# Moving the last block's first stages between two feed-forward stages, and splitting late weight sums, in a fast-multiplication transformer block

## The chip, the cores and the metric

The kernel runs on one core of a Trainium2 chip. A core has five engines, each with a queue of its own that it works through in order: TensorE (PE, matrix products; its weight loads are the rows PEld), VectorE (DVE), ScalarE (ACT), GpSimd (POOL) and SyncE (SP, which here only issues DMAs). Engines wait for each other by semaphores. Arithmetic is in float32. The metric is the device time of one execution in microseconds (us).

## The reference

The input `x` is 2 rows of 2048 tokens with 512 features, and a condition vector for each row. The condition gives six vectors for each row (shift, scale and gate of two sub-layers):

```
emb = silu(t) @ ada_w + ada_b
shift_msa, scale_msa, gate_msa, shift_mlp, scale_mlp, gate_mlp = split(emb, 6)
norm = _ln(x) * (1 + scale_msa) + shift_msa
h = gelu(norm @ ssm_w1 + ssm_b1)            # exact gelu, 512 -> 512
x = x + gate_msa * (h @ ssm_w2 + ssm_b2)    # 512 -> 512
norm2 = _ln(x) * (1 + scale_mlp) + shift_mlp
hf = gelu(norm2 @ ff_w1 + ff_b1)            # tanh gelu, 512 -> 1024
x = x + gate_mlp * (hf @ ff_w2 + ff_b2)     # 1024 -> 512
```

## The kernel before

**Tiles and stages.** The 4096 tokens are cut into 8 blocks of 512 tokens (`NBLK`), four for each row of `x` (`PER_B`). A block goes through four products, which I call stages: hA (norm 1 times ssm_w1, class `First`), oA (times ssm_w2, `residual`), hC (norm 2 times ff_w1, `Second.products`) and oC (times ff_w2, `residual_in_leaves`). hA(7) is that stage of block 7, the last.

**Fast multiplication.** hA and oA are done as 2x2 blocks with seven products instead of eight, P1 to P7, in the order P1 P5 P6 P2 P7 P3 P4 (`CARRIED`); each has eight matmuls of 128x256. The operands of some products are sums: four sums make a "second operand" or a "first operand" (`sums_of_second`, `sums_of_first`, all recorded at line 348). nS is such a set from the normed input of hA, hSA from hA's output, hSC from hC's output, fw_t from the ff weight. hC has 26 products (`HK_P`) over 20 "forms", sums of blocks of the normed input (`sums_of_registers`, L919). oC cuts most of its seven products once more into seven "leaves" (rounds R0 to R6), whose operands are further sums: sums24, sums35, sums7 (`leaf_sums`) and the leaves of the weight (`leaves_of_weight`: P23, P4, P5, P7). A product's result in PSUM is added to its place by DVE (L735 in oA, L785 and L834 in oC, L998 in hC) or first copied by ACT (L995 in hC). A PSUM bank is used again only after it was read: that is how PE comes to wait for DVE or ACT. Biases get into PSUM ahead of the products by ACT copies ("seeds", L445 and L447).

**Norms.** A norm of a block is a chain over five engines: statistics (DVE, L512 and L513, four pieces), scales (POOL, eight small operations, L548 to L566, the last gives `nmr`), four normals (ACT, L580), four turns (DVE transposes into `blocks`, L591), 16 DMAs of 64 KB that finish the transpose (`move`, L600), and four modulates (ACT, L623, from `moved`). Norm 1 works in the place of x, so x is loaded again (`load_x`, L203) for the residual.

**The order of the work** is written out by hand. `hook(hooks, places, ops)` puts operations of the other engines behind a named product of a stage (behind product number n in hC); each engine then does them in that order:

```
    def hook(hooks, places, ops):
        for n, op in enumerate(ops):
            hooks.setdefault(places[min(n, len(places) - 1)], []).append(op)
```

With the order `CARRIED` the places of oA and hA are named by position: P1, P2, P6, P5, P7, P3, P4 mean behind the first, second, ... seventh product. The hooks of a stage stand in the queues between what the stage's own products need, so a sum that is hooked into oA stands ahead of the adds that follow it.

**The loop** (L1285 on) runs over i = 1 to 7. For each i it does, in PE's order: hC(i), oA(i+1), oC(i), hA(i+2); what would belong to a block past the last is left out. Block 7 therefore has hA(7) after oC(5), oA(7) after hC(6), and hC(7), oC(7) at the end. For block i+2, norm 1's normals are hooked at products 15, 17, 19, 21 of hC(i), its turns two products later, its moves at 23 (all on SP), its modulates behind the fifth product of oA(i+1), its nS sums in oC(i) on POOL. For block i+1, norm 2 runs through oA(i+1) (statistics), and oC(i) (scales, normals, turns, moves half on SP and half on ACT, modulates), and its 20 forms are made by POOL after oC(i), beside hA(i+2). In the iteration i = 6 there is no hA(8): the forms of block 7 are hooked late into oC(6) (`late_form`), the first six on DVE and 14 on POOL, and two of the four modulates are POOL's.

**Weights.** The ff weight is multiplied by the row's gate (`weight_of_second`, fold L396) and its sums are formed. For the first row, eight of its sums (`later`) are made by DVE inside oA(2) in the iteration i = 1. When the second row begins, in iteration i = 3, the weight is loaded again in two halves (`load_half`), folded by DVE in hA(5), and summed by DVE and POOL in hA(5), hC(4), oA(5) and oC(4).

**Storage.** Tiles of 1 MB (`big_tile`) come from a pool of seven; x, the normed inputs, hA, hClo and hChi are such tiles.

## Time and profile before

| | |
|---|---|
| three timed runs | 592.53, 594.62, 594.88 us; median 594.62 |
| the profiled execution | 594.65 us, its span 592.9 us |
| mean granted TensorE clock | 0.996 |
| PE busy | 582.0 us |
| DVE, ACT, POOL busy | 415.1, 261.9, 434.4 us |
| steady iterations (start of hA to start of hA) | 193.16, 262.33, 331.48: 69.17 and 69.15 us |
| the iteration with the new weight | 331.48 to 402.06: 70.58 us |
| the next | 402.06 to 471.22 (start of hA(7)): 69.16 us |
| hC(7) starts | 541.66 us |
| PE's last product ends | 588.3 us |

The profiled execution lies at the median. Its trace gives each instruction of each engine with its start and duration in microseconds from the span's start, and in brackets how long the engine stood idle before it and what ended the wait. A row such as `x8` joins eight instructions that follow each other; its duration then runs to the end of the last, which overlaps the next row a little, because matmuls are pipelined. A line number is that of the line which recorded the instruction; a helper such as L348 serves many tiles, so the names of the output and the input tiles tell which sums they are.

### The profile page before, as it was taken

To read this page: it belongs to the slowest core of one execution; us is meant where nothing else is said; L and a number is where in the kernel's file an instruction comes from. 1 tells how busy PE (TensorE), PEld (TensorE's weight loads), DVE (VectorE), ACT (ScalarE), POOL (GpSimd) and SP (SyncE) were. 2 spreads that over 40 slices of the span, in tenths; PEclk is the share of its full clock that TensorE was granted. 3 is DMA by queue.
4 is the path that set the end of the run, shared out by engine and by line. 5 is a ranking of instruction groups with operands and counts; after the bars stand their busy time and mean duration, and the time that the engine had idled before them with its cause. 6 is when DMAs were issued, how large, how long until landed. Compare 5 with 4: busy or idle time off the path is not lost.

```text
span 592.9 us, 9491 instructions
## 1 busy us (share of the span) xinstructions
PE 582.0 (98%) x3303; PEld 517.3 (87%) x3303; DVE 415.1 (70%) x750; ACT 261.9 (44%) x477; POOL 434.4 (73%) x522
## 2 busy tenths in 40 slices
PE   9999999999989999999999999999999999998996
PEld 5888888888879888998889988898889988897896
DVE  4978888897867365685756578874665626587666
ACT  2234457305533546435742588226474255312430
POOL 1875359999976938969788789997679693755460
PEclk9999999999989999999999999999999999999999
DMA  8990333302305402372033820233120420013002
GB/s 318 395 384 10 86 72 82 98 36 106 72 2 143 153 9 62 99 221 81 2 89 69 287 72 22 51 85 149 52 53 19 127 89 0 1 32 111 1 1 71
DMA packets 25243, 56.49 MB, mean 95 GB/s; under 512 B 4672, under 2 KB 5740, under 8 KB 23532
## 3 DMA queue, kind: packets, MB, share of 16 engines
q1 hardware_dynamic: 21472, 51.15, 26.9%
q10 hardware_dynamic: 3724, 4.75, 3.3%
q8 instruction: 26, 0.43, 0.3%
q14 instruction: 21, 0.17, 0.1%
HBM read 32.80 MB, written 8.40 MB: 69 GB/s over the span
## 4 chain that ended last, share of the span: by engine, by line
PE 83%; DVE 8%; DMA 4%; issue 1%; POOL 1%; ACTq 1%; ACT 1%; SPq 0%; DVEq 0%; POOLq 0%
PE px_hC L981 9%; PE py_hA L475 9%; PE py_oA L475 8%; PE py_hC L981 7%; PE py_oC L774 7%; PE pv_hC L981 7%; PE pl_oC_P_y L820 6%; PE pv_hA L475 4%; PE pl_oC_P_v L820 4%; PE pv_oA L475 4%; PE py_oC L475 2%; PE py_hC L475 2%; DMA ada<-in_L_cond_ada_w_dram 2%; PE pl_oC_P_x L820 2%; PE px_oA L475 2%; PE px_hA L475 2%
## 5 line engine op out<-in xcount | busy, mean ns | idle before, releaser
L348 POOL TENSOR_TENSOR hSC<-hClo,hChi 128x512 f32<-128x512 f32 (+1 forms) x17 | 20.4, 1207 | 42.1 <-ACT hChi L976 24.7
L623 ACT ACTIVATE nT<-nT,mod,mod 128x512 f32<-128x512 f32 x30 | 22.0, 803 | 56.0 <-DMA nT<-blocks 32.5
L919 POOL TENSOR_TENSOR forms<-forms 128x256 f32<-128x256 f32 x55 | 40.8, 741 | 4.7 <-DVE forms L919 1.5
L512 DVE BATCH_NORM_STATS2 st<-x 128x6 f32<-128x512 f32 x60 | 40.6, 676 | 5.1 <-DMA x<-in_x_dram 4.8
L981 PE MATMUL py_hC<-forms,fw 128*128 128x256 f32 x168 | 41.1, 380 | 0.4 <-DVE hClo L998 0.4
L998 DVE TENSOR_TENSOR hClo<-hClo,py_hC 128x512 f32<-128x512 f32 x42 | 28.5, 685 | 15.7 <-ACT hClo L995 9.7
L580 ACT ACTIVATE nT<-x,nmr,rstd 128x512 f32<-128x512 f32 x32 | 24.0, 806 | 35.1 <-POOL nmr L566 35.1
L981 PEld LDWEIGHTS py_hC<-forms,fw 128*128 128x128 f32 x168 | 31.8, 190 | 5.2 <-DVE hClo L998 0.8
L591 DVE STREAM_TRANSPOSE blocks<-nT 128x512 f32<-128x512 f32 x32 | 22.3, 707 | 18.8 <-ACT nT L580 18.8
L623 ACT ACTIVATE x<-x,mod,mod 128x512 f32<-128x512 f32 x24 | 17.6, 803 | 37.5 <-DMA x<-blocks 37.5
L998 DVE TENSOR_TENSOR hChi<-hChi,pv_hC 128x512 f32<-128x512 f32 x35 | 23.2, 681 | 9.8 <-PE pv_hC L981 8.1
L919 POOL TENSOR_TENSOR forms<-nT,forms 128x256 f32<-128x256 f32 x39 | 28.6, 754 | 1.0 <-DVE forms L919 0.5
L981 PE MATMUL px_hC<-forms,fw 128*128 128x256 f32 x112 | 27.9, 380 | 0.1
L976 ACT ACTIVATE hClo<-hClo,colsT 128x256 f32<-128x256 f32 x56 | 25.3, 499 | 5.0 <-DVE hClo L998 4.8
L475 PE MATMUL py_oA<-w,hA 128*128 128x256 f32 x112 | 26.5, 380 | 0.5 <-DVE x L735 0.5
L834 DVE TENSOR_TENSOR x<-pl_oC_P_y,x 128x256 f32<-128x256 f32 (+1 forms) x66 | 24.7, 375 | 2.4 <-PE pl_oC_P_y L820 0.9
L735 DVE TENSOR_TENSOR x<-py_oA,x 128x512 f32<-128x512 f32 x26 | 17.8, 686 | 11.8 <-PE py_oA L475 11.3
L976 ACT ACTIVATE hChi<-hChi,colsT 128x256 f32<-128x256 f32 x56 | 25.1, 497 | 1.9 <-DVE hChi L998 1.9
L774 PE MATMUL py_oC<-fw,hClo 128*128 128x256 f32 x112 | 26.0, 386 | 0.0
L995 ACT ACTIVATE hClo<-px_hC 128x512 f32<-128x512 f32 x21 | 12.5, 597 | 30.2 <-PE px_hC L981 25.8
L697 DVE TENSOR_TENSOR hA<-py_hA,hA 128x512 f32<-128x512 f32 x7 | 4.8, 690 | 30.0 <-PE py_hA L475 19.2
L774 PE MATMUL py_oC<-fw_s,hSC 128*128 128x256 f32 x112 | 25.3, 379 | 0.0
(340 smaller groups left out, 1792.8 us busy)
## 6 DMA issues: line engine op xcount, KB each, us to landing
x<-in_x_dram SPq DMA_DIRECT2D x13, 1024.0 KB
out_dram<-x SPq DMA_DIRECT2D x14, 512.0 KB
ada<-in_L_cond_ada_w_dram SPq DMA_DIRECT2D x6, 1024.0 KB
x<-blocks SPq DMA_DIRECT2D x96, 64.0 KB
nT<-blocks SPq DMA_DIRECT2D x72, 64.0 KB
fw<-in_L_cond_ff_w_dram SPq DMA_DIRECT2D x2, 2048.0 KB
nT<-blocks ACTq DMA_DIRECT2D x56, 64.0 KB
w<-in_L_cond_ssm_w_dram SPq DMA_DIRECT2D x3, 1024.0 KB
```

The lines of the kernel that those rows point to most:

```text
L475: nc.tensor.matmul(ps[b][j * apart][:, j, :], lhs(p, j, k), rhs(p, j, k), start=(fresh and j * (not apart) == 0 and k == 0), stop=(p in (" ...
L512: nc.vector.bn_stats(st, xs[self.i][:, c, :])
L580: nc.scalar.activation(t, x_c, AF.Identity, bias=self.nmr[:, c : c + 1], scale=self.rstd[:, c : c + 1])
L591: nc.vector.transpose(self.bl[:, :, :, c, :].rearrange("p m k q -> p k m q"), self.nT[:, c, :].rearrange("p (k m q) -> p k m q", k=KD, m=C),)
L623: nc.scalar.activation(dst, src, AF.Identity, bias=shift, scale=scale)
L774: yield lambda j=j, k=k: nc.tensor.matmul(ps[BANK[p]][:, j, :], hops(p, j, k), wops[p][:, k, :], start=False, stop=(k == kdim - 1), skip_g ...
L820: nc.tensor.matmul(t[:, n, :], hops.leaves[p][f][:, k, :], leaf_wops[p][f][:, k, :], start=room not in started, stop=(f in ("P2", "P3", "P ...
L834: nc.vector.tensor_tensor(d, src, d, ALU.add)
L919: eng.tensor_tensor(reg[d], reg[a], reg[b], ALU.add if f == "+" else ALU.subtract)
L976: nc.scalar.activation(h, h, AF.Gelu_apprx_tanh, bias=fb1T[:, m : m + 1])
L981: nc.tensor.matmul(ps[b][:, j, :], fa[ra][:, j * P : (j + 1) * P], fb[rb].rearrange("p a (c q) -> p c a q", q=Q), start=(fresh and j == 0) ...
L998: nc.vector.tensor_tensor(dest(d), dest(d), ps[b], op)
```

## The change

1. In iteration i = 5 (`ahead`), hA(7) is put between oA(6) and oC(5), and oA(7) between oC(5) and hC(6). PE's order is then hC(5), oA(6), hA(7), oC(5), oA(7), hC(6), oC(6), hC(7), oC(7). With it, norm 1 of block 7 moves: normals at products 9, 11, 13, 15 of hC(5) instead of 15 to 21, turns and the 16 moves (SP) with them, modulates behind the first product of oA(6) instead of the fifth. The four nS_7 sums are DVE's in oA(6), behind its third, fourth and fifth products, in a big tile (before: POOL's in oC(5)). The seeds of oC(5) stand in hA(7), x_7's second load and block 7's hSA sums (POOL) in oC(5), where also the seeds of oA(7) are.
2. Norm 2 of block 7: two statistics in oA(7) and two in hC(6), scales, normals, turns and moves in hC(6) (all 16 moves on SP), modulates behind P1 of oC(6), all on ACT. The 20 forms of block 7 follow there, all on POOL.
3. In the iterations i = 6 and 7 (`alone`), the second half of the hSC sums and sums24 are DVE's, sums35 and sums7 POOL's; the most part stands behind P1 of oC.
4. Iteration i = 1: four of the eight late weight sums stay in oA(2), the other four go behind P1 of oC(1), and the normals there come at R0.
5. The second row's ff weight: its second half is loaded first; hA(5) folds that half, makes two of its sums, and folds the first half, nine operations behind its fourth product and one behind its fifth; the rest follows in hC(4), oA(5) and oC(4) as before.

The list of PE's matmuls stays the same, in another order.

```diff
-        def summed(self, eng):
+        def summed(self, eng, in_big=False):
...
+        ahead, alone = i + 3 == NBLK, not nx2
...
-        if nxt:
+        if nx2:
             hook(hooks, (3,), [lambda: load_x(i + 1)])
             hook(hooks, (1, 2, 3, 4), hA[i + 1].summed(nc.gpsimd))
+        elif nxt:
+            hook(hooks, (1, 3), last_stats[2:])
+            hook(hooks, (3,), [n2[i + 1].scales])
+            hook(hooks, (15, 17, 19, 21), [lambda c=c: n2[i + 1].normal(c) for c in range(C)])
+            hook(hooks, (17, 19, 21, 23), [lambda c=c: n2[i + 1].turn(c) for c in range(C)])
+            hook(hooks, (23,), [n2[i + 1].move])
...
-            at = (12, 14, 16, 18) if i == 1 else (15, 17, 19, 21) if five else (18, 19, 20, 21)
+            at = (12, 14, 16, 18) if i == 1 else (9, 11, 13, 15) if ahead else (15, 17, 19, 21)
...
         if fold:
-            hook(hooks, (0,), fold[:1])
-            hook(hooks, (5, 8), fold[1:5])
-            hook(hooks, (8, 13), fold[5:7])
-            hook(hooks, (13,), fold[9:13])
+            hook(hooks, (5, 8), fold[:4])
+            hook(hooks, (13,), fold[6:10])
...
+        hC_sums = hC.summed(1, nc.vector if alone else nc.gpsimd)
+        hook(hooks, EARLY, hC_sums[: 2 if alone else 4])
+        engs = (nc.vector if alone else nc.gpsimd, nc.gpsimd, nc.gpsimd)
...
+            hook(hooks, ("P1",) if ahead else ("P7",), n1[i + 2].moved())
+            if ahead:
+                hook(hooks, ("P6", "P5", "P7"), n1[i + 2].summed(nc.vector, True))
             if i == 1:
-                hook(hooks, ("P1", "P1", "P2", "P2", "P6", "P6", "P5", "P5"), later)
+                hook(hooks, ("P1", "P1", "P2", "P6"), later[:4])
             if fold:
-                hook(hooks, ("P1", "P2", "P6", "P5"), fold[8:9] + fold[7:8] + later[:2])
+                hook(hooks, ("P1", "P2", "P6", "P5"), fold[5:6] + fold[4:5] + later[:2])
...
             residual(f"oA_{i + 1}", i + 1, hA[i + 1], w2_ops, KD // 2, hooks, order=CARRIED)
+            if ahead:
+                hooks = {}
+                hook(hooks, ("P2", "P6"), oC_seeds)
+                hA[i + 2] = First(i + 2, n1[i + 2].ops, hooks, CARRIED, on_act=("P6", "P5"))
...
-        leaf_fold, fold = fold and later[2:], None
+        leaf_fold, fold = (fold or i == 1) and later[2 if fold else 4 :], None
...
+        if alone:
+            hook(hooks, ("P1",), hC_sums[2:] + sums7[:2] + sums35[:2] + sums24[:2] + sums7[2:] + sums35[2:])
+            hook(hooks, ("R0", "P6"), sums24[2:])
...
-            hook(hooks, ("P1", "R0") if leaf_fold else ("P1", "P1", "R0") if nx2 else ("P1",), [...normal...])
+            hook(hooks, ("R0",) if leaf_fold else ("P1", "P1", "R0"), [...normal...])
...
+        if ahead:
+            hook(hooks, ("P1",), [lambda: load_x(i + 2)])
+            hook(hooks, ("P1", "P2"), hA[i + 2].summed(nc.gpsimd))
+            hook(hooks, ("R4", "P4"), [lambda p=p: seed(f"oA_{i + 2}", gb[2], p) for p in range(2)])
...
-            moved = n2[i + 1].moved((None,) if nx2 else (None, nc.gpsimd))
-            hook(hooks, ("R2",) if nx2 else ("P5", "R2", "P5", "R2"), moved)
+            hook(hooks, ("R2",) if nx2 else ("P1",), n2[i + 1].moved())
...
-                def late_form(n):
-                    if n == 0:
-                        late["ops"] = form((nc.vector,) * 6 + (nc.gpsimd,) * 14)
-                    late["ops"][n]()
-                hook(hooks, ("P7",), [lambda n=n: late_form(n) for n in range(len(HK_B))])
+                hook(hooks, ("P1",), form((nc.gpsimd,)))
...
         if refold5:
+            load_half("fw2", fw2, fw2_sb, 1)
             load_half("fw2", fw2, fw2_sb, 0)
-            load_half("fw2", fw2, fw2_sb, 1)
...
-            fold += ops["P23"] + ops["P4"]
+            folds, fold = fold[4:8] + ops["P23"][:2] + fold[:4], fold[8:] + ops["P23"][2:] + ops["P4"]
...
-            hook(hooks, ("P5", "P5", "P5", "P7", "P7", "P3", "P4"), fold[:7])
-            fold = fold[7:]
+            hook(hooks, ("P5",) * 9 + ("P7",), folds)
...
-        if nx2:
+        if ahead:
+            n2[i + 2] = Norm(i + 2, 2)
+            last_stats = n2[i + 2].stats()
+            hook(hooks, ("P3", "P4"), last_stats[:2])
+            residual(f"oA_{i + 2}", i + 2, hA[i + 2], w2_ops, KD // 2, hooks, order=CARRIED)
+        elif nx2:
             hA[i + 2] = First(i + 2, n1[i + 2].ops, hooks, CARRIED, on_act=("P6", "P5"))
```

More of the change, by code (lines that the diff above doesn't have):

```diff
@@ L643, in registers @@
             ]
-        def summed(self, eng):
-            s = thirds(sums.tile([P, 3, C, KD // 2, HT // C], F32, tag="s", name=f"nS{self.name}"))
+        def summed(self, eng, in_big=False):
+            if in_big:
+                flat = big_tile(f"nS{self.name}").rearrange("p a b -> p (a b)")[:, : 3 * KD // 2 * HT]
+                s = thirds(flat.rearrange("p (s a k r) -> p s a k r", s=3, a=C, k=KD // 2))
+            else:
+                s = thirds(sums.tile([P, 3, C, KD // 2, HT // C], F32, tag="s", name=f"nS{self.name}"))
             h = self.nT.rearrange("p a (k h r) -> p a k h r", k=KD, h=2)
@@ L1288 @@
             hook(hooks, (1, 1, 3, 5, 7), unread_stats)
-        if nxt:
+        if nx2:
             hook(hooks, (3,), [lambda: load_x(i + 1)])
             hook(hooks, (1, 2, 3, 4), hA[i + 1].summed(nc.gpsimd))
+        elif nxt:
[4 more added lines that the diff above has]
+            hook(hooks, (23,), [n2[i + 1].move])
         if nx2 and i > 1:
             hook(hooks, (7,) if unread_stats else (5,), [n1[i + 2].scales])
-        if nxt:
+        if nx2:
             hook(hooks, (20, 24), [lambda p=p: seed(f"oA_{i + 1}", gb[2], p) for p in range(2)])
@@ L1318 @@
         hooks = {}
-        hook(hooks, EARLY, hC.summed(1, nc.gpsimd if nxt else nc.vector))
-        engs = (nc.vector if last else nc.gpsimd, nc.gpsimd, nc.gpsimd if nx2 or last else nc.vector)
+        hC_sums = hC.summed(1, nc.vector if alone else nc.gpsimd)
+        hook(hooks, EARLY, hC_sums[: 2 if alone else 4])
+        engs = (nc.vector if alone else nc.gpsimd, nc.gpsimd, nc.gpsimd)
         sums24, sums35, sums7 = hC.leaf_sums(nxt, nx2, five, engs)
-        if last:
-            hook(hooks, ("P5",), sums35[:2] + sums7[:2] + sums35[2:] + sums7[2:])
+        if alone:
+            pass
         else:
@@ L1327 @@
             sums35 = sums35[:2] + sums7[:2] + sums35[2:] + sums7[2:]
-        elif five and not last:
-            hook(hooks, ("P7",) if nx2 else ("P5", "P7", "P7", "P3"), sums7)
-        if nxt:
-            if nx2:
-                hook(hooks, ("P7",), n1[i + 2].moved())
+        elif nx2:
+            hook(hooks, ("P7",), sums7)
+        if nx2:
+            hook(hooks, ("P1",) if ahead else ("P7",), n1[i + 2].moved())
+            if ahead:
+                hook(hooks, ("P6", "P5", "P7"), n1[i + 2].summed(nc.vector, True))
             if i == 1:
-                hook(hooks, ("P1", "P1", "P2", "P2", "P6", "P6", "P5", "P5"), later)
+                hook(hooks, ("P1", "P1", "P2", "P6"), later[:4])
             if fold:
-                hook(hooks, ("P1", "P2", "P6", "P5"), fold[8:9] + fold[7:8] + later[:2])
-            hook(hooks, ("P2", "P6"), [lambda p=p: seed(f"oC_{i}", gb[5], p, five) for p in range(2)])
+                hook(hooks, ("P1", "P2", "P6", "P5"), fold[5:6] + fold[4:5] + later[:2])
+            oC_seeds = [lambda p=p: seed(f"oC_{i}", gb[5], p, five) for p in range(2)]
+            if not ahead:
+                hook(hooks, ("P2", "P6"), oC_seeds)
             n2[i + 1] = Norm(i + 1, 2)
@@ L1341 @@
             residual(f"oA_{i + 1}", i + 1, hA[i + 1], w2_ops, KD // 2, hooks, order=CARRIED)
+            if ahead:
+                hooks = {}
+                hook(hooks, ("P2", "P6"), oC_seeds)
+                hA[i + 2] = First(i + 2, n1[i + 2].ops, hooks, CARRIED, on_act=("P6", "P5"))
         else:
@@ L1350 @@
             hook(hooks, ("P5",), [lambda: load_x(i + 3)])
-        if last:
-            hook(hooks, ("P1",), sums24[:2])
-            hook(hooks, ("P6",), sums24[2:])
-        if nxt:
+        if alone:
+            hook(hooks, ("P1",), hC_sums[2:] + sums7[:2] + sums35[:2] + sums24[:2] + sums7[2:] + sums35[2:])
+            hook(hooks, ("R0", "P6"), sums24[2:])
+        if nx2:
             if leaf_fold:
@@ L1359 @@
             hook(hooks, ("P1",), sums35)
-            hook(hooks, ("P1", "R0") if leaf_fold else ("P1", "P1", "R0") if nx2 else ("P1",), [lambda c=c: n2[i + 1].normal(c) for c in range(C)])
+            hook(hooks, ("R0",) if leaf_fold else ("P1", "P1", "R0"), [lambda c=c: n2[i + 1].normal(c) for c in range(C)])
             turns = ("P2",)
@@ L1370 @@
             hook(hooks, ("P1",), [lambda: load_w("w2", w2, w2_sb)])
-        if nx2:
+        if ahead:
+            hook(hooks, ("P1",), [lambda: load_x(i + 2)])
+            hook(hooks, ("P1", "P2"), hA[i + 2].summed(nc.gpsimd))
+            hook(hooks, ("R4", "P4"), [lambda p=p: seed(f"oA_{i + 2}", gb[2], p) for p in range(2)])
+        elif nx2:
             hook(hooks, ("P1", "P2"), n1[i + 2].summed(nc.gpsimd))
         if nxt:
-            moved = n2[i + 1].moved((None,) if nx2 else (None, nc.gpsimd))
-            hook(hooks, ("R2",) if nx2 else ("P5", "R2", "P5", "R2"), moved)
+            hook(hooks, ("R2",) if nx2 else ("P1",), n2[i + 1].moved())
         refold5 = (i + 1) % PER_B == 0 and nxt
@@ L1382 @@
         if nxt:
-            late = {}
             def form(engs):
@@ L1427 @@
             hook(hooks, ("P7", "P7", "P4") if refold5 else ("P5", "P7", "P3", "P4"), st)
-        if nx2:
+        if ahead:
[3 more added lines that the diff above has]
+            residual(f"oA_{i + 2}", i + 2, hA[i + 2], w2_ops, KD // 2, hooks, order=CARRIED)
+        elif nx2:
             hA[i + 2] = First(i + 2, n1[i + 2].ops, hooks, CARRIED, on_act=("P6", "P5"))
```

## The prediction

> **What bounds the kernel now.** I read the shares and slices first, then PE's waits, then PE's timeline at each wait, then the other engines' timelines there. (hC, oA, oC, hA below are the four stages of a block's work; oC(5) is that of block 5.)

> From the page:
> ```profile
> PE 582.0 (98%) x3303; PEld 517.3 (87%) x3303; DVE 415.1 (70%) x750; ACT 261.9 (44%) x477; POOL 434.4 (73%) x522
> ...
> PE   9999999999989999999999999999999999998996
> ```
> PE sets the time, and almost without holes. Its list of products only changes order, so the change can win only where PE stands still. PE's waits are few:
> ```profile
> PE py_oA L475 <- DVE x L735: 2.3, 2, 1.9
> ...
> PE py_hC L981 <- DVE forms L919: 1.1, 1, 1.1
> PE pv_hC L981 <- POOL forms L919: 0.6, 1, 0.6
> PE py_hC L981 <- DVE hClo L998: 0.4, 1, 0.4
> ```
> These are total, count and longest, in us: three places, A (first line), C (second and third), B (fourth).

> A wait costs more than its idle time, so I measure places by stage starts. Eight 128x256 products start every 1.726 us, sixteen every 3.453. A steady iteration (hA start 262.33 to 331.48) is 69.15 us: hC 22.45, oA 12.09, oC 22.53, hA 12.09.

> **A**, oA(2). PE's timeline:
> ```profile
> 161.55 1.97 PE L475 MATMUL py_oA<-w,hA 128*128 128x256 f32 x8 [0.48 <-DVE x L735]
> 163.35 1.89 PE L475 MATMUL pv_oA<-w,hSA 128*128 128x256 f32 x8
> 167.10 3.09 PE L475 MATMUL py_oA<-w_s,hA 128*128 128x256 f32 x8 [1.86 <-DVE x L735]
> 169.98 4.25 PE L774 MATMUL py_oC<-fw,hClo 128*128 128x256 f32 x16
> ```
> The first columns are start and duration. The two late starts lose 0.65 and 2.02; then eight products take 2.88 (+1.15) and sixteen 4.09 (+0.64): 4.46. Check: hC(1) start to hA(3) start is 193.16-131.54 = 61.62, against 57.07 for a steady hC+oA+oC: 4.55. I take 4.5. The slow products have their reason in the stretches (seventh number: granted clock):
> ```profile
> 166.00:168.00 2.00, 0.90 (x4) 0.82 (x5) 1.97 (x4) 0.79 (x2) 2.00 (x3) 0.96 0.00 0
> 168.00:170.00 2.00, 2.00 (x7) 1.55 (x6) 0.55 (x2) 0.21 (x1) 1.92 (x4) 0.50 0.00 0
> 170.00:172.00 2.00, 2.00 (x8) 1.66 (x7) 1.74 (x4) 0.00 (x0) 0.43 (x1) 0.69 0.00 0
> ```
> So 2.34 us of idle cost 1.8 more by the clock. PE waited because DVE's adds of the products (L735) stood behind eight weight sums:
> ```profile
> 164.96 1.48 DVE L348 TENSOR_TENSOR fw_t<-fw,fw_t 128x256 f32<-128x256 f32 x1
> 166.37 0.68 DVE L735 TENSOR_TENSOR x<-py_oA,x 128x512 f32<-128x512 f32 x1
> ```

> **C**, start of hC(7):
> ```profile
> 541.66 1.10 PE L981 MATMUL py_hC<-forms,fw_s 128*128 128x256 f32 x4 [1.12 <-DVE forms L919]
> 543.39 1.10 PE L981 MATMUL pv_hC<-nT,fw_s 128*128 128x256 f32 x4 [0.62 <-POOL forms L919]
> ```
> Forms start at 539.3, since the DMAs land at 537.4 (normals at 525.42). Starts run 2.6 late in all; the clock stays 1.00.

> **B**, block 4's new ff weights: hC(4) loses 0.25+0.57+0.1, oC(4) 0.44: 1.4.

> Profiled: span 592.9, time 594.65, 1.75 outside the span; the median 594.62 is 0.03 below, so the sum is made on 594.65.

> **The change, part by part.**

> *Weight sums split (A).* Four of the eight DVE sums stay in oA(2), in the rows 0.42, 1.38, 1.07, 1.49, the fourth behind the third add. The third product's add then ends at 160.1, before 160.9 when it is needed; px's at 162.2, the next py's at 163.5, before 164.35. No stall, no slow clock: **-4.5**. The other four (0.89+1.37+0.89+1.48 = 4.6) go to oC(1) behind its first read; DVE has a 2.28 hole there (175.03 to 177.31), and the next reads leave 1.5 by my chain. If that cover is gone up to 1.5 returns; I take 0.

> *Refold of block 4 (B).* 10 of the DVE ops for the weight go into hA(5), among them two 128x512 sums; the one that took 2.00 at 352.47 leaves hC(4): -0.67 (0.57+0.1). Normals at one place in oC(4): -0.15. But hA(5)'s add at 340.41 now stands behind folds (0.62 apart, from 334.96) and two sums, and ends near 342.0 where its product starts at 341.84: +0.25 (0 to 1), and ACT half a us later, +0.1. **-0.4** (-0.9 to +0.5).

> *Block 7's ssm stages earlier; its forms by POOL (C).* PE's order becomes hC(5) oA(6) hA(7) oC(5) oA(7) hC(6) oC(6) hC(7) oC(7). Norm 2 of block 7 then runs through hC(6) (normals at products 15 to 21, turns 17 to 23, 16 moves on SP at 23). SP needs 10.0 to 10.8 for 16 moves, and hC start to the last modulate (L623) is 37.0 to 37.6 in steady iterations, so 14.6 to 15.1 into oC(6). Then POOL makes 20 forms: 14.55 in row 470.29 to 484.84. The first form that PE could miss is the eleventh: the second half of the third product wants it 1.73+0.86 = 2.6 into hC(7), 25.1 after oC(6) starts; it is done at 15.1+8.15 = 23.25. Margin 1.9: C goes, **-2.6**. Its cover is POOL being free at 13.3 to 13.7; each us that POOL or the landing is later than 1.9 costs one. hC(6) takes two extra norm statistics on DVE (0.69+0.18 each): +0.1 (0 to 0.3). The sums of blocks 6 and 7 (DVE and POOL) reach their reads with over 2 us by the rows of 566 to 571: 0 (-0.2 to 0.2); the 4.6 behind PE's end stays.

> *New wait D1, in hC(5).* Norm 1 of block 7 moves up six products. ACT's first two normals now wait for POOL:
> ```profile
> 425.44 0.23 POOL L566 TENSOR_SCALAR nmr<-nmr 128x4 f32<-128x4 f32 x1
> ```
> Queued behind them on ACT is this read of PSUM:
> ```profile
> 425.57 0.60 ACT L995 ACTIVATE hClo<-px_hC 128x512 f32<-128x512 f32 x1 [1.50 <-PE px_hC L981]
> ```
> Two normals (0.70 apart) from 425.67 put it at 427.1 to 427.7; PE wants the bank at 427.10. **+0.7** (0 to 0.9).

> *New wait D2, in oA(6).* The fourth turn ends near 432.15 (436.25 before). SP issues the 16 moves, then ACT modulates:
> ```profile
> 436.28 10.79 SPq L600 DMA_DIRECT2D x<-blocks  x16
> ```
> ```profile
> 448.59 2.93 ACT L623 ACTIVATE x<-x,mod,mod 128x512 f32<-128x512 f32 x4 [8.18 <-DMA x<-blocks]
> ```
> Issue to modulate is 12.3 here, 11.6 and 11.9 in the two iterations before: modulate starts at t = 443.8 to 444.5. Before, nothing waited on it for 20 us. Now DVE's first sum nS_7 stands in oA(6) behind the third product's add and waits for two modulates (1.45), and behind it stand px's add, the second sum (four modulates), and the py add that PE's last product needs (planned 447.65, D1 in it). DVE sums of 128x512 take 0.69 (566.43) with POOL idle and 1.35 and 1.65 (569.69, 571.08) beside POOL, which is busy here from 438.5 to 452; I take 1.35. PE starts at t+1.45+1.35+0.69+1.35+0.69 = t+5.5 = 449.3 to 450.0: +1.7 to 2.4. With sums of 0.69 and the adds at 0.60: +0.8; with 2.00 (352.47): +3.3. I take **+1.9**. Else the earlier stage passes these queues: POOL loses nS_7's four sums and gets block 7's hSA sums in oC(5) in their place; SP issues x_7's reload (one DMA, free to go once hA(7) has ended) ahead of nT_6's moves, of which SP's eight took 6.10 at 459.69, with 7.5 to spare at hC(6) (eleventh form 478.4, wanted 485.9); ACT's seeds for oA(7) come 0.4 or more before use: 0, up to 0.3 each where a margin is thinner than I read it.

> [...]

> **Sum**: -4.5-0.4-2.6+0.7+1.9+0.1 = -4.8: 589.8 us.

> **Rivals.**
> 1. *D2 starts the clock drop.* For it: A's 1.86 wait had it, 1.8 more. Against: C's 1.12+0.62 had none. 591.6. [...]
> 2. *D2 is small*: sums at 0.69 and an earlier landing, stall 0.5 or less: 588.4; with B at its best and D1 nothing 587.
> 3. *The split does not remove A*: the four sums and later normals in oC(1) hold DVE's reads there, a wait takes the wait's place: some 594. The same time if C's landing slips instead and D2 comes with the clock drop.
> 4. *Slower*: block 7's moves land no earlier than before. The turns are earlier only if ACT's normals, interleaved with PSUM reads, get through; if t stays at 448.59, PE starts at 454.1, 6.5 late, and the clock adds 1.8: 594.65-6.7+8.3 = 596.2. It decides from t = 447.0 on; past 450 the time is over 597.6.
> 5. *The change does not do what it says*: PE still waits on forms at hC(7), since POOL is held by its sums (C stays, 592.4).

> **How the numbers follow.** Half a per cent, 3.0 us, is about what a measurement of this kernel tells from no change: faster is under 591.65, slower over 597.6. Chances: forecast (588 to 591.6) 0.47, small D2 0.15, clock drop 0.17 (half of it under 591.65), A or C kept 0.12, slower rival 0.09 (0.05 of it over 597.6). Faster 0.47+0.15+0.08 = 0.70, same 0.25, slower 0.05. The low end is B at -0.9, D1 and D2 at nothing: 594.65-4.5-0.9-2.6 = 586.6; the high end D1 0.9, D2 3.3, clock 1.8, B +0.5, hC(6) 0.3: 594.3. Outside lie the slower rival and part of the kept gains.

> **What would show it.** A: no PE wait on L735 near 161 to 167, clock 1.00 there, hC(1) to hA(3) near 57.1. C: hC(7) starts without waits on L919. B: hA(5)'s last product 0.2 to 0.3 late, no 0.4 wait on L998 behind it. D1: a wait of PE on ACT's L995 near hC(5)+13. D2: PE's last oA(6) product waits on DVE L735, ended by L623 and L348, and the clock behind it. The prediction is wrong if PE shows waits in oC(1), at hA(7) or at oA(7), which are priced at nothing, or if a modulate of block 7 starts past 447.

## The result

The changed kernel takes **589.37 us** (median of 6 runs, 588.97 to 589.57); the kernel before, run with it, 594.23 (6 runs, 592.53 to 594.88). The ratio is 0.9923, 95% interval 0.9908 to 0.9937. The forecast was 589.8, with a range of 586.6 to 594.3. The profiled execution takes 589.1, its span is 587.3.

I read the profile after in the same order. The page's shares and slices:

```profile
PE 579.2 (99%) x3303; PEld 516.4 (88%) x3303; DVE 415.9 (71%) x752; ACT 263.2 (45%) x479; POOL 428.4 (73%) x518
...
PE   8999999999999999999999999999999999999997
```

PE does the same products in 2.8 us less of busy time, most of it the slow clock that is gone (1.7 at A), and its slices have no hole left between the first and the last. PE's waits (total, count, longest, in us):

```profile
PE py_oA L475 <- DVE x L739: 1.1, 1, 1.1
PE px_hC L985 <- ACT hClo L999: 0.5, 1, 0.5
```

The lines of before for A, B and C are gone (L735 of before is L739 here, 998 is 1002, and so on). Two new ones have come, both in the iteration that was rebuilt. Place A in PE's timeline, and the clock there (the seventh number):

```profile
160.88 1.89 PE L475 MATMUL py_oA<-w,hA 128*128 128x256 f32 x8
162.60 1.89 PE L475 MATMUL pv_oA<-w,hSA 128*128 128x256 f32 x8
164.33 1.89 PE L475 MATMUL py_oA<-w_s,hA 128*128 128x256 f32 x8
166.06 3.62 PE L778 MATMUL py_oC<-fw,hClo 128*128 128x256 f32 x16
```

```profile
168.00:170.00 2.00, 2.00 (x13) 1.82 (x12) 1.50 (x5) 0.00 (x0) 1.92 (x4) 1.00 0.00 0
170.00:172.00 2.00, 2.00 (x20) 1.97 (x19) 1.90 (x5) 0.41 (x2) 1.75 (x4) 1.00 0.03 8
```

Starts 1.73 apart, no idle time, clock 1.00. Place C, the start of hC(7):

```profile
537.26 1.03 PE L985 MATMUL py_hC<-forms,fw_s 128*128 128x256 f32 x4
538.13 1.03 PE L985 MATMUL pv_hC<-nT,fw_s 128*128 128x256 f32 x4
538.99 1.89 PE L985 MATMUL px_hC<-forms,fw 128*128 128x256 f32 x8
```

The two new waits. D1 in hC(5), on PE and on ACT:

```profile
422.21 1.13 PE L985 MATMUL px_hC<-forms,fw 128*128 128x256 f32 x4 [0.49 <-ACT hClo L999]
423.18 1.03 PE L985 MATMUL pv_hC<-nT,fw_s 128*128 128x256 f32 x4
424.28 2.00 PE L985 MATMUL py_hC<-forms,fw 128*128 128x256 f32 x8
```

```profile
420.16 1.52 ACT L580 ACTIVATE x<-x,nmr,rstd 128x512 f32<-128x512 f32 x2 [1.63 <-POOL nmr L566]
421.58 0.57 ACT L999 ACTIVATE hClo<-px_hC 128x512 f32<-128x512 f32 x1
```

ACT waits 1.63 us for POOL's `nmr`, does two normals, and only then reads the bank that PE wants at 421.56. D2 in oA(6), on ACT, DVE and PE:

```profile
438.74 2.93 ACT L623 ACTIVATE x<-x,mod,mod 128x512 f32<-128x512 f32 x4 [4.03 <-DMA x<-blocks]
```

```profile
440.35 1.06 DVE L348 TENSOR_TENSOR nS<-x 128x512 f32<-128x512 f32 x1 [2.05 <-ACT x L623]
441.33 0.68 DVE L739 TENSOR_TENSOR x<-px_oA,x 128x512 f32<-128x512 f32 x1
441.93 1.16 DVE L348 TENSOR_TENSOR nS<-x,nS 128x512 f32<-128x512 f32 x1
443.01 0.68 DVE L739 TENSOR_TENSOR x<-py_oA,x 128x512 f32<-128x512 f32 x1
```

```profile
443.74 1.99 PE L475 MATMUL py_oA<-w_s,hA 128*128 128x256 f32 x8 [1.06 <-DVE x L739]
```

This is the chain as the prediction wrote it down: modulate, sum, add, sum, add, product. PE wanted to start at 440.79+1.73 = 442.52.

**Where the time went, by stages.** Lengths from one stage's first product to the next one's, in us. The first column of times is what they are with no wait. The kernels of the four other columns come below; "end" is from oC(7)'s start to the end of the span.

| stages | no wait | before | after | split alone | refold alone | move alone | no split |
|---|---|---|---|---|---|---|---|
| A: oA(2)+oC(1) | 34.62 | 39.16 | 34.62 | 34.62 | 37.48 | 37.47 | 37.47 |
| B: hC(4)+oC(4) | 44.99 | 46.41 | 45.42 | 46.38 | 45.46 | 46.45 | 45.46 |
| D1: hC(5) | 22.45 | 22.45 | 23.55 | 22.44 | 22.45 | 23.89 | 23.68 |
| D2: oA(6) | 12.09 | 12.09 | 13.42 | 12.09 | 12.08 | 13.41 | 13.42 |
| C: oC(6)+hC(7) | 44.98 | 47.59 | 44.98 | 48.26 | 47.36 | 44.99 | 44.98 |
| end | | 27.47 | 27.59 | 27.42 | 27.43 | 27.54 | 27.63 |

Before to after: -4.54, -0.99, +1.10, +1.33, -2.61, +0.12 make -5.59; the spans differ by 5.6. The medians differ by 4.86, and the experiments show why.

### The profile page after: what moved, and what is told of

It reads as the page before. It is cut to its first block, busy times and chain, and to the rows that moved or that the text cites. A ratio compares the mean times of both kernels' runs of the same rounds, so it can differ in the third digit from the quotient of the medians.

```text
span 587.3 us, 9483 instructions
## 1 busy us (share of the span) xinstructions
PE 579.2 (99%) x3303; PEld 516.4 (88%) x3303; DVE 415.9 (71%) x752; ACT 263.2 (45%) x479; POOL 428.4 (73%) x518
## 4 chain that ended last, share of the span: by engine, by line
PE 73%; POOL 11%; DVE 5%; DMA 5%; issue 3%; SPq 1%; ACT 1%; POOLq 0%; DVEq 0%
PE py_oA L475 7%; PE px_hC L985 7%; PE py_oC L778 7%; PE py_hA L475 7%; PE pl_oC_P_y L824 6%; PE py_hC L985 6%; PE pv_hC L985 6%; PE pl_oC_P_v L824 4%; PE pv_oA L475 4%; PE pv_hA L475 3%; PE py_oC L475 2%; PE py_hC L475 2%; DMA ada<-in_L_cond_ada_w_dram 2%; PE pl_oC_P_x L824 2%; POOL forms L923 2%
## 5 line engine op out<-in xcount | busy, mean ns | idle before, releaser
L348 POOL TENSOR_TENSOR hSC<-hClo,hChi 128x512 f32<-128x512 f32 (+1 forms) x16 | 19.2, 1205 | 40.8 <-ACT hChi L980 36.0
L623 ACT ACTIVATE nT<-nT,mod,mod 128x512 f32<-128x512 f32 x32 | 23.4, 802 | 55.6 <-DMA nT<-blocks 40.1
L623 ACT ACTIVATE x<-x,mod,mod 128x512 f32<-128x512 f32 x24 | 17.6, 802 | 33.8 <-DMA x<-blocks 33.8
L923 POOL TENSOR_TENSOR forms<-nT,forms 128x256 f32<-128x256 f32 x42 | 30.6, 748 | 1.7 <-PE pl_oC_P_v L824 1.3
L923 POOL TENSOR_TENSOR forms<-nT 128x256 f32<-128x256 f32 x14 | 10.4, 740 | 27.6 <-ACT nT L623 20.7
L475 PE MATMUL py_oA<-w,hA 128*128 128x256 f32 x112 | 26.5, 379 | 0.0
L980 ACT ACTIVATE hChi<-hChi,colsT 128x256 f32<-128x256 f32 x56 | 25.1, 496 | 2.0 <-DVE hChi L1002 1.9
L739 DVE TENSOR_TENSOR x<-py_oA,x 128x512 f32<-128x512 f32 x26 | 17.9, 687 | 11.4 <-PE py_oA L475 10.8
L999 ACT ACTIVATE hChi<-py_hC 128x512 f32<-128x512 f32 x14 | 7.6, 593 | 40.9 <-POOL forms L923 21.0
```

The source lines that it names most:

```text
L475: nc.tensor.matmul(ps[b][j * apart][:, j, :], lhs(p, j, k), rhs(p, j, k), start=(fresh and j * (not apart) == 0 and k == 0), stop=(p in (" ...
L623: nc.scalar.activation(dst, src, AF.Identity, bias=shift, scale=scale)
L923: eng.tensor_tensor(reg[d], reg[a], reg[b], ALU.add if f == "+" else ALU.subtract)
L980: nc.scalar.activation(h, h, AF.Gelu_apprx_tanh, bias=fb1T[:, m : m + 1])
```

## The experiments

**1. The parts alone.** Four kernels on one chip. *Split alone*: the kernel before with part 4.

```diff
...
-                hook(hooks, ("P1", "P1", "P2", "P2", "P6", "P6", "P5", "P5"), later)
+                hook(hooks, ("P1", "P1", "P2", "P6"), later[:4])
...
-        leaf_fold, fold = fold and later[2:], None
+        leaf_fold, fold = (fold or i == 1) and later[2 if fold else 4 :], None
...
-            hook(hooks, ("P1", "R0") if leaf_fold else ("P1", "P1", "R0") if nx2 else ("P1",), [...normal...])
+            hook(hooks, (("R0",) if i == 1 else ("P1", "R0")) if leaf_fold else ("P1", "P1", "R0") if nx2 else ("P1",), [...normal...])
...
```

> The kernel before with the split of block 1's late weight sums alone (four stay in oA(2), four go behind P1 of oC(1), normals at R0). Theory: the parts act in places of their own and add up, so this one takes all of A: -4.5 us, 589.7; oA(2) 12.1 and oC(1) 22.5 us, clock 1.00 at 166 to 172. Rival 1: the four sums meet the norm in oC(1) and only part of A goes, 591 or more. Rival 2: the slow clock at 168 to 172 has another reason than the two waits; then it stays, and the gain is 2.7: 591.5.

Measured: 590.4 us, ratio 0.9932 (0.9909 to 0.9956). oA(2) is 12.08 and oC(1) 22.54, the clock 1.00: the stall went as expected. C is 0.7 longer here than in the profile of before (first wait 1.8 us in place of 1.1), with nothing edited there; in the four profiles that still have C it is 47.36 to 48.26.

*Refold alone*: the kernel before with part 5, the normals of oC(4) at R0 among it.

```diff
...
-            hook(hooks, ("P1", "R0") if leaf_fold else ("P1", "P1", "R0") if nx2 else ("P1",), [...normal...])
+            hook(hooks, ("R0",) if leaf_fold else ("P1", "P1", "R0") if nx2 else ("P1",), [...normal...])
...
+            load_half("fw2", fw2, fw2_sb, 1)
             load_half("fw2", fw2, fw2_sb, 0)
-            load_half("fw2", fw2, fw2_sb, 1)
...
+            folds, fold = fold[4:8] + ops["P23"][:2] + fold[:4], fold[8:] + ops["P23"][2:] + ops["P4"]
...
+            hook(hooks, ("P5",) * 9 + ("P7",), folds)
...
```

> The kernel before with the new order of the second row's weight alone (half 1 first, two sums in hA(5), normals at R0 in oC(4)). Theory: -1.0 us, 593.2, from hC(4) (23.44 to 22.9) and oC(4) (22.97 to 22.5), hA(5) unchanged at 12.1. Rival: part of that was the split's doing through earlier timing (DVE sums beside another POOL operation), then hA(5) shows a late last product of 0.2 to 1 us and the gain is 0.4 or less.

Measured: 593.64, ratio 0.9992 (0.9974 to 1.0011), which does not tell 1.0 from nothing. The stages do: B is 45.46 in place of 46.41, hA(5) 12.10.

*Move alone*: the changed kernel with parts 4 and 5 taken back, both diffs read backwards:

```diff
...
-                hook(hooks, ("P1", "P1", "P2", "P6"), later[:4])
+                hook(hooks, ("P1", "P1", "P2", "P2", "P6", "P6", "P5", "P5"), later)
...
-            hook(hooks, ("P5",) * 9 + ("P7",), folds)
+            hook(hooks, ("P5", "P5", "P5", "P7", "P7", "P3", "P4"), fold[:7])
...
```

> The changed kernel with the split and the refold both undone, so that only block 7's stages, its forms and the sums of blocks 6 and 7 are changed against the kernel before. Theory: C -2.6, D1 +1.1, D2 +1.3, the last oC and its tail +0.1: -0.1 us, 594.1, the same as before. Rival: the move is what makes the kernel faster, at least -2.5 us, 591.7 or less.

Measured: 593.49, ratio 0.9985 (0.9966 to 1.0004): the same as before. By stages C gives 2.60, D1 takes 1.44, D2 1.32. The rebuilt iteration by itself wins next to nothing; its gain is eaten by the two waits that it brings.

*No split*: the changed kernel with part 4 alone taken back (the first two lines of that diff, and `leaf_fold` for the fold only).

> The changed kernel with the split alone undone (all eight sums in oA(2)). Theory: +4.5 us, 593.9, with the two waits on the adds and the clock of 0.5 to 0.7 back. Rival: the parts do not add up, +3 or less.

Measured: 592.17, ratio 0.9974 (0.9958 to 0.9990): +2.8, not +4.5. The two waits are back word for word, but the slow clock is not:

```profile
161.63 1.97 PE L475 MATMUL py_oA<-w,hA 128*128 128x256 f32 x8 [0.48 <-DVE x L739]
163.43 1.89 PE L475 MATMUL pv_oA<-w,hSA 128*128 128x256 f32 x8
167.18 1.99 PE L475 MATMUL py_oA<-w_s,hA 128*128 128x256 f32 x8 [1.86 <-DVE x L739]
169.01 1.24 PE L778 MATMUL py_oC<-fw,hClo 128*128 128x256 f32 x5
```

The last product of oA(2) takes 1.83 to the next start here and 2.88 in the profile of before, behind the same 0.48 and 1.86 us of idle time. So the waits cost 2.85 each time (the three profiles without a drop have 37.47 to 37.48 at A), and the drop of the clock, 1.7 more, comes in some executions only; of the five profiles with A, two have it, the one of before and that of the last experiment below (39.14 at A). It shows in the times too. The kernel before ran 50 times beside these kernels; sorted by the mean clock of the execution:

| mean clock | runs | times, us |
|---|---|---|
| 0.998 to 1.000 | 20 | 592.4 to 594.0 |
| 0.995 to 0.997 | 22 | 594.1 to 595.2 |
| 0.994 | 8 | 596.1 to 596.7 |

The three groups lie some 1.6 us apart, which fits no drop, one, or two. Refold alone, which keeps A and C, falls into the same three groups: 3, 3 and 4 of its 10 runs, some 1.4 us apart. The kernel with neither A nor C (the changed one) has 0.998 to 1.000 in all 6 runs. With A but not C, two of 10 (no split) and three of 10 (move alone) are slow by one step; with C but not A, one of 7. So C's waits seem to start it too now and then; no profile caught that. The shares are rough: 5 of 20 and one of 7 would give some 18 of 50 runs with a drop where A and C come together, not 30. What I had taken for a fixed part of A is a chance, and the split takes it away.

The traces show more of that chance. In the clock records of each of the 14 profiles of this case the clock changed only at points 3.41 us apart, and these points lay elsewhere against the program in each execution. In the profile of before it fell to 0.50 at 167.84, rose at 171.25 and fell again, behind PE's last product, at 591.10, which is 123 steps of 3.413 after 171.25; in that of the changed kernel it fell once, at 586.43, 170 such steps after its first record at 6.16. The drops that met products lasted 3.41 us (before; the last experiment below, 168.40 to 171.81) or 6.83 (the slower rival below), and 3.41 us at half the clock cost 1.7. Now take PE's idle time in each interval between two points that begins at a clock of 1.00. In all 12 intervals inside the spans with 2.06 us or more (11 of them at the end, as PE runs out of work: 2.79 before, 3.34 after), the clock fell at the interval's end; with 1.83 or less it never did (before and after had 1.67 at most). A's long wait of 1.86 lies between: where it was whole inside one interval, the clock fell in two profiles (before, and the last experiment) and stayed in one (no split); in the other two a point cuts it into 1.34 and 0.52, or 1.37 and 0.49, and the clock stayed. This was read from the profiles at hand; no run was made to test it.

**2. The two new waits.** Two edits of the changed kernel, and both together. *Scales first*: POOL does block 7's scales ahead of the hSA sums.

```diff
+            if ahead:
+                hook(hooks, (0,), [n1[i + 2].scales])
             hook(hooks, (1, 2, 3, 4), hA[i + 1].summed(nc.gpsimd))
...
-        if nx2 and i > 1:
+        if nx2 and i > 1 and not ahead:
```

> The changed kernel with the scales of block 7's norm 1 ahead of the hSA sums on POOL in hC(5), not behind them. Theory of D1: the two normals wait for nmr at hC(5)+11.5, and the PSUM read behind them is late; with nmr at about hC(5)+6.4 the wait of PE on ACT L999 goes and hC(5) is 22.45 again (23.55 in the changed kernel): -1.1 us, 588.3; D2 stays at 1.3, since turns and PE both come earlier. Rival: the normals themselves, on ACT between two reads of PSUM, cost it whenever they are; then hC(5) stays at 23 or more and the time at 589 or more.

Measured: 588.21, ratio 0.9913 (0.9899 to 0.9927); hC(5) 22.45, oA(6) 13.40. D1 was the wait for POOL and not the normals themselves.

*nS on POOL*: the four sums of D2 on POOL, ahead of sums24.

```diff
+            if ahead:
+                hook(hooks, ("P5",), n1[i + 2].summed(nc.gpsimd, True))
             hook(hooks, ("P5",), sums24)
...
-            if ahead:
-                hook(hooks, ("P6", "P5", "P7"), n1[i + 2].summed(nc.vector, True))
```

> The changed kernel with the four nS_7 sums on POOL in oA(6), behind hSC's and ahead of sums24, not on DVE. Theory of D2: DVE's adds stand behind sums that wait for the modulates, so without them PE's last product of oA(6) is on time: oA(6) 12.1 in place of 13.4, -1.3 us, 588.05; POOL's sums end 5 us later, which oC(5) does not feel. Rival: POOL's waiting (2 us for the modulates) and its later sums24, sums7 and scales come out in oC(5) or hC(6) as a new wait, and 0.5 or more comes back.

Measured: 588.07, ratio 0.9907 (0.9892 to 0.9922); oA(6) 12.08, hC(5) 23.46, and oC(5) and hC(6) keep 22.54 and 22.44. POOL, four sums later, holds nobody up.

> The two edits together on the changed kernel: scales of block 7's norm 1 ahead of the hSA sums, and nS_7 on POOL. Theory: D1 and D2 are separate waits in a row, so both go: -2.4 us, 587.0, faster than the changed kernel and the kernel before. Rival: they share a cause (late modulates), then the gain is that of one alone, 588 to 588.3.

Measured: 586.89, ratio 0.9893 (0.9878 to 0.9908). hC(5) is 22.44 and oA(6) 12.09; no wait of PE is listed behind its first 20 us. The two waits were separate.

**3. The slower rival, made on purpose.** The changed kernel with block 7's normals where the other iterations have them.

```diff
-            at = (12, 14, 16, 18) if i == 1 else (9, 11, 13, 15) if ahead else (15, 17, 19, 21)
+            at = (12, 14, 16, 18) if i == 1 else (15, 17, 19, 21) if ahead else (15, 17, 19, 21)
```

> The changed kernel with the normals of block 7's norm 1 at products 15 to 21 of hC(5), as in the other iterations, so that the modulates come late; everything else as changed. This is the slower rival made on purpose. Theory: D1 goes (-1.1), the modulates start 34.4 after hC(5) starts, at 443.05, PE's last product of oA(6) at 448.05 in place of 441.4: a wait of 6.6 in place of 1.3; 593.6, and by the kernel before's slow clock behind 1.9 us of idle 1.8 more, 595.4. Rival: PE waits for something else, less than 3 us in all, 591 or less.

Measured: 595.31, ratio 1.0029 (1.0016 to 1.0042): slower than the kernel before. D1 is gone (hC(5) 22.45), and oA(6) takes 20.14. PE's timeline and the stretches behind the wait:

```profile
448.36 3.78 PE L475 MATMUL py_oA<-w_s,hA 128*128 128x256 f32 x8 [6.05 <-DVE x L739]
451.93 2.69 PE L475 MATMUL py_hA<-x,w 128*128 128x256 f32 x8
```

```profile
446.00:448.00 2.00, 0.00 (x0) 0.00 (x0) 2.00 (x4) 0.61 (x1) 1.09 (x1) 0.68 0.00 0
448.00:450.00 2.00, 1.64 (x4) 1.37 (x5) 2.00 (x4) 0.00 (x0) 0.00 (x0) 0.50 0.00 0
450.00:452.00 2.00, 2.00 (x7) 1.55 (x6) 0.98 (x3) 0.00 (x0) 0.00 (x0) 0.50 0.00 0
```

The product is 6.2 late, then two groups of eight products take 3.57 and 2.53 in place of 1.73: 2.6 more by the clock, which is at 0.50 from 446.71 to 453.54, twice 3.41 us. All 10 runs have a mean clock of 0.995 or less. The normals, turns and moves of one norm, put six products later, turn a gain of 5 us into a loss.

**4. The end.** In the changed kernel oC(7) is 23.37 long, 0.5 more than before, with no wait of PE listed. DVE has no wait there from 572.34 to its last add, which ends at 583.62, and this stands near its start:

```profile
572.94 1.78 DVE L348 TENSOR_TENSOR forms<-hChi,forms 128x512 f32<-128x512 f32 x1
574.64 0.41 DVE L838 TENSOR_TENSOR x<-pl_oC_P_y,x 128x256 f32<-128x256 f32 x1
```

It is the fourth sums24, hooked at P6. On top of the kernel of both edits I put it at R0, or on POOL.

```diff
-            hook(hooks, ("R0", "P6"), sums24[2:])
+            hook(hooks, ("R0",) if last else ("R0", "P6"), sums24[2:])
```

> The kernel with both new waits taken out (scales first, nS_7 on POOL), and in the last oC the fourth sums24 at R0 with the third, not behind P6. Theory of the end: from P6 on DVE works without a gap, and the sum of 1.78 us there holds the adds that PE and the last stores wait for; at R0 DVE has 0.8 us of idle time, so the tail gets shorter by about 1: 586.0. Rival: the sum at R0 holds the adds of the second round instead, and PE loses there what it gains: 586.9.

Measured: 586.07, ratio 0.9852 (0.9832 to 0.9873). oC(7) is 22.70, and from oC(7)'s start to the end of the span 26.95 in place of 27.53.

```diff
+            if last:
+                sums24[3:] = hC.leaf_sums(nxt, nx2, five, (nc.gpsimd,) * 3)[0][3:]
```

> The same kernel with that fourth sum on POOL, which has nothing left to do after its own sums. Theory of the end: DVE's adds start 1.7 us earlier, PE's late starts of 0.5 in the last oC go and the adds behind PE's last product with them: 0.8 less, 586.1. Rival: the end is set by PE and the last stores alone; then 0.2 or less.

Measured: 586.07, ratio 0.9853 (0.9829 to 0.9878), the same stage lengths to 0.05. Both take the same 0.6 off by stages (0.8 by the medians, which were taken on different chips), so it is the sum's place in DVE's last stretch that cost, and not which engine does it. These two are the fastest kernels of the study, 3.3 us below the changed one.

**5. What missed or stayed small.** *Moves of block 7's norm 2 later*, to see how thin C's margin is:

```diff
-            hook(hooks, (23,), [n2[i + 1].move])
...
+            if not nx2:
+                hook(hooks, ("P1",), [n2[i + 1].move])
             hook(hooks, ("R2",) if nx2 else ("P1",), n2[i + 1].moved())
```

> The changed kernel with the 16 moves of block 7's norm 2 behind P1 of oC(6), not behind product 23 of hC(6), some 3.8 us later. Theory of C: forms start at oC(6)+15.0 with 1.9 us to spare, so the first 1.9 cost nothing (and 0.5 are free, since POOL is not done before), and what is over comes out as a wait of PE on forms at hC(7): +1.4 us, 590.8. Rival: the forms are not what PE needs there, or POOL's sums set the time: 589.4.

Measured: 589.32. The edit did not do what I meant. SP issues the 16 moves 0.3 us before oC(6) starts, as in the changed kernel: they wait for the fourth turn, and a hook fixes the order in a queue, not a time. The forms started 15.0 us into oC(6), as before. So this says nothing of the margin; D1 was 1.70 in that profile.

*Normals of block 5 at R0 alone*, on the kernel before:

```diff
-            hook(hooks, ("P1", "R0") if leaf_fold else ("P1", "P1", "R0") if nx2 else ("P1",), [...normal...])
+            hook(hooks, ("R0",) if leaf_fold else ("P1", "P1", "R0") if nx2 else ("P1",), [...normal...])
```

> The kernel before with the four normals of block 5's norm 2 at R0 of oC(4) and nothing else changed. Theory: the whole 0.44 that oC(4) lost goes by this alone, oC(4) 22.54 in place of 22.97, hC(4) unchanged at 23.44. Rival: the weight sums that move to hA(5) and hC(4) are needed too: oC(4) 22.8 or more. The time of one run does not tell 0.4.

One profile: oC(4) 22.54, hC(4) 23.46; its time was 594.41, at clock 0.996. All of oC(4)'s 0.44 goes by the place of the normals, as expected. It is also the second profile that caught A's drop: the clock is at 0.50 from 168.40 to 171.81, and A is 39.14.

## Why the prediction was right, step by step

- **A, -4.5.** In the profile it was made on: -4.54, right to 0.05. But only 2.85 of it is fixed. The other 1.7 is the drop of the clock, which that execution had and 20 of 50 do not. The profiled execution and the median of the runs shown had one drop, so the sum came out right against them; against a run without a drop it would have been 1.7 too much. The 1.8 that the prediction put on the clock is this chance priced as a fixed cost. The four sums in oC(1) cost nothing, and less than I had priced: 0.41 to 0.42 each, beside POOL's small operations of the scales, where they took 0.89 to 1.48 beside POOL's sums in oA(2) (see D2).
- **C, -2.6.** -2.61. The forms start at 529.73, 15.0 into oC(6), and the eleventh is done at 537.91 with 539.85 wanted: 1.94 to spare, predicted 1.9. That the number fits is in part luck. The prediction let the last modulate set the forms' start and had POOL free at 13.3 to 13.7; the modulates ended at 529.27 (14.5), and it was POOL, busy with its sums until 15.0, two of them 1.72 long beside DVE's, that held the forms. The margin was not tested, see above.
- **B, -0.4.** Mis-sized: -0.99 (the prediction's own terms make -0.47). The wait in hA(5) that I charged with 0.25 did not come: two weight sums took 0.82 and 1.10, and the add ended at 337.04, 0.24 before its product. The 0.1 for a later ACT did come: its first read in hC(4) starts 2.29 into the stage in place of 2.16, and hC(4) gave 0.55 of the 0.67. And oC(4) gave 0.44 where I had put 0.15 on the normals; the last experiment shows that they were all of it.
- **D1, +0.7.** +1.10, outside its own 0 to 0.9; 1.0 to 1.7 in the kernels that have it. The cause was right (scales first takes it away whole). The size was too small because I priced the first late start only, 0.65: the next reads of PSUM and adds of DVE come late too, and the products behind lose 0.1, 0.1 and 0.24 more.
- **D2, +1.9.** +1.33. The place, the chain and the modulates' start (438.74; predicted 443.8 to 444.5 in a time scale 5.54 later, so 438.3 to 439.0) were right. The sums took 1.06 and 1.16, not 1.35, and D1's larger share had already moved PE's wish by 0.4. POOL's rows beside them:

```profile
439.58 1.27 POOL L348 TENSOR_TENSOR forms<-forms,hChi 128x512 f32<-128x512 f32 x1
440.81 1.72 POOL L348 TENSOR_TENSOR hChi<-hChi 128x512 f32<-128x512 f32 x1
442.50 1.71 POOL L348 TENSOR_TENSOR forms<-hChi,forms 128x512 f32<-128x512 f32 x1
```

DVE's first sum starts at 440.35, with 0.50 of a POOL sum left, and takes 0.37 more than the 0.69 it takes alone; the second starts with 0.60 left and takes 0.47 more. POOL's sums at 440.81 and 442.50 start with 0.60 and 0.59 of DVE's left and take 0.45 and 0.44 more than 1.27. So in these four the sum that started second took its own time and what was left of the other's, less 0.13 to 0.15. The rows behind the prediction's 1.35 and 1.65 fit that too (0.81 and 1.10 left), so 1.35 was the length of one overlap and no fixed cost. DVE's add from PSUM at 441.33, inside POOL's 1.72, kept its 0.68. Why the second takes longer no run here shows.
- **Rivals 2, 3 and 5.** D2 was between the forecast and the small one, with sums nearer to 1.1 than to 0.69. The split did remove A, alone too, so rival 3 fell; hC(7) starts without a wait, so rival 5 fell. Of the signs that were to show the prediction wrong, none came: PE has no wait in oC(1), at hA(7) or at oA(7), and the modulates start 2.7 before the limit (447, which is 441.5 here).
- **Rival 1, the clock behind D2.** It did not come: 0.998 or more in the 6 runs of the changed kernel and in the 9 of the two variants that keep D2 without A. One idle stretch of 1.06 us did not start it here; 0.48 and 1.86 did in some executions, and 6.05, by a mean clock of 0.995 or less, in all 10.
- **Rival 4, slower.** It was priced at 596.2 for a modulate that starts as late as in the kernel before. Made on purpose, it gave 595.31 as median and 596.26 in the profiled execution.
- **Small terms.** The +0.1 for hC(6) did not come (22.45 against 22.44). Not seen was the end, +0.12: I had it at nothing, and it hid 0.6 that could be had there.
- **The sum, -4.8.** The profiles differ by 5.6: B and D2 came out 0.6 better each, D1 0.4 worse. That the medians differ by 4.86, as forecast, is luck: by their times (592.53, 593.07, 593.99), three of the six runs of the kernel before had no drop.

What stays open: why the clock fell in two of the three profiles with A's wait whole between two points and not in the third, whether C's waits start a drop too, and how thin C's margin is.

## What to carry to other kernels

A wait costs what it delays, so price it by the starts of the products behind it; and look at several executions, because the clock may add to it in some and not in others (1.7 us here), so that taking the wait away also makes the times agree better. A sum on DVE that runs beside sums on POOL had no fixed length here (128x512: 0.69 us alone, up to 2.00 beside them): look at what is left of the other's when it starts. When a step is moved ahead of its old place, write down for each engine what is now queued behind its first waiting instruction: both new waits here were of that kind. One was taken away by changing the order of two groups on POOL, the other by giving the waiting sums to an engine that nobody waits for, and together that was worth 2.5 us, half of what the change gave. An engine without a gap in the last stage can set the end (0.6 us here), even where the profile marks no wait.
